# Two graph layers on one core: Q's first product ahead of fc_w's fourth, one block read by ScalarE's queue, and a reordered prologue

## The chip, the cores and the metric

The kernel runs on 1 core of one Trainium2 chip. The metric is the device time of one execution in microseconds. Three runs of the kernel before took 2433.7, 2435.32 and 2435.53 us; their median is 2435.32.

## The reference, cut to what matters

Two graph layers follow each other, on x of 64 x 256 x 512 and a 0/1 adjacency of 64 x 256 x 256, all in float32.

```python
# layer 0
feat_proj = feats @ fc_w.T + fc_b
q = feat_proj @ q_w.T + q_b;  k = feat_proj @ k_w.T + k_b
masked = (q + k.T) + (1 - adj) * -1e9
atten = softmax(leaky_relu(masked, 0.01))
x = atten @ feat_proj + feats
# layer 1, 8 heads of 64
Q, K, V = (x @ W + b for W, b in ((W_q, b_q), (W_k, b_k), (W_v, b_v)))
scores = Q K^T / 8 + (a_i + c_j + b_g) + log(adj + 1e-9)
out = softmax(scores) V + x          # a = x @ w_g[:512], c = x @ w_g[512:]
```

## The kernel before

**Groups and passes.** The 64 graphs are taken two at a time: a group is 2 graphs, 512 tokens, in four tiles of 128 tokens. `step(a, f, n)` is called 32 times and interleaves three groups: layer 1's attention of group a, layer 0 and the projections of group f, and the loads and the scalar logits of group n. Inside it, strings such as `F("pf.p4 pf.sum_10 send:1:0 fetch:1:0")` name methods in the order in which they are issued. The whole runs under a manual schedule, so on each engine the order of the program is the order of execution. There are 31 steps with attention and layer 0 (`attention_and_layer_0`), and a first one without attention (`features_first`).

**Products by seven.** The projections (class `Product`, L360) multiply 512 x 512 by 512 x 512 in 2 x 2 blocks with seven products in place of eight (Winograd's form). For this the blocks of the weights and of the tokens are added and subtracted first: `blocks_of_weights` (L285 to L288, on VectorE, once per weight) and `xsum:n` (L325) for the tokens. p1 to p7 are eight matmuls each; `keep_1` and its like copy a partial result from PSUM to SBUF on ScalarE, and `sum_00` to `sum_11` finish a block of the output on VectorE. Q's products are pq, K's pk, V's pv; pf is fc_w's product in layer 0, whose sums (L446) also scale by the softmax's denominators and add the residual. In pf the last product p4 adds to the PSUM bank of p7 after `sum_11` has read it.

**The way of x1.** Layer 0's result x1 stands with tokens on partitions and is needed with features on partitions. Four blocks (o, k) go through DRAM: `send:o:k` transposes 32 x 32 pieces on VectorE (L661) and writes xt to xd (L665), `fetch:o:k` reads it back into x1T with four transfers (L673), each write and read issued by SyncE. SyncE takes its instructions in order and waits for a write to land before it issues the reads of that block. Product pq.p1 needs block (0,0); `xsum:0` needs (0,1), `xsum:1` and `xsum:2` need (1,1), `xsum:3` and pq.p2 need (1,0); pq.p6 needs the first two sums.

**PSUM.** Pool ps has four banks for all products, sums and transposes; pool psc has two pairs of banks for the scores. A bank is given again when its last reader is done: pk.p1, for instance, takes the bank that the second oT copy (ScalarE, L774) reads.

**The prologue.** fc_w is loaded in one transfer by ScalarE's queue, q_w, k_w and fc_b as columns (`column`, L127: 512 pieces of 4 bytes each) by SyncE, then q_b, k_b, x and adj of group 0 and the three weights. `row_of_x` (L231) makes rows q_w fc_w and k_w fc_w on all partitions, from which VectorE takes the logits as dot products with x (`dot_q`, `dot_k`, L461). `transposed_weights` transposes fc_w (L148). `features_first` then transposes x (L591), computes feat_proj tile by tile (fp, L603), the softmax's weights e (L531 to L536), their sums (L544), and x1 (x1p, L621, L625). `constants_of_projections` (pc, L259) adds fc_b's part to Q's and V's bias; its four products of 32 rows lie in four column tiles of TensorE.

Of the kernel before, what the change touches and what calls it, by code (L numbers as in the profile page):

```python
# [10 lines left out]
F32 = mybir.dt.float32  # L11
I32 = mybir.dt.int32
AF = mybir.ActivationFunctionType
ALU = mybir.AluOpType
# [3 lines left out]
P = 128  # L18
# [7 lines left out]
def kernel(  # L26
# [133 lines left out]
    def fast():  # L160
        main = ExitStack()
        with main:
# [47 lines left out]
                nc.gpsimd.memset(ones[:, n, n : n + 1], 1.0)  # L210

            fc_nat = one.tile([P, T, D], F32, tag="xT", name="fc_nat")
            nc.scalar.dma_start(fc_nat, fc_w.rearrange("(c p) h -> p c h", p=P))
            qw_col = column(q_w.rearrange("a h -> (a h)"), "qw_col")
            kw_col = column(k_w.rearrange("a h -> (a h)"), "kw_col")
            fcb_col = column(fc_b, "fcb_col")
            qb = row(q_b, "qb")
            kb = row(k_b, "kb")
            x_0, adj_0 = load_x(0), load_adj(0)
            wq_sb = weights(W_q, "wq", wts)  # L220
            wk_sb = weights(W_k, "wk", wts)
            wv_sb = weights(W_v, "wv", wts)
            bq_col = column(b_q, "bq_col")
            wgc_row = row(w_g[D : 2 * D], "wgc_row")
            bv_col = column(b_v, "bv_col")

            def row_of_x(col, dst, name):

                pw = bank(name)
                for oc in range(NC):  # L230
                    nc.tensor.matmul(  # L231
                        pw, lhsT=col[:, oc : oc + 1].to_broadcast([P, P]), rhs=fc_nat[:, oc, :],
                        start=(oc == 0), stop=(oc == NC - 1),
                    )
                nc.scalar.copy(dst, pw)

            def constant():

# [14 lines left out]
            def constants_of_projections():  # L253


                pc = bank("pc")[:, 0:HALF]
                for n, (w, o) in enumerate(((wq_sb, 0), (wq_sb, 1), (wv_sb, 0), (wv_sb, 1))):
                    for c in range(NC):
                        nc.tensor.matmul(  # L259
                            pc[ts(n, RS), :], lhsT=fcb_col[:, c : c + 1].to_broadcast([P, RS]),  # L260
                            rhs=w[:, c, o * HALF : (o + 1) * HALF],
                            start=(c == 0), stop=(c == NC - 1), tile_position=(0, n * RS),
                        )
                rows = one.tile([P, HALF], F32, tag="st", name="pc_rows")
                nc.scalar.copy(rows, pc)
                pt = bank("pct")
                for m in range(2):
                    nc.tensor.transpose(pt[:, ts(m, P)], rows[:, ts(m, P)], ident)
                cols = pt[:, 0 : 2 * P].rearrange("p (m n r) -> p n m r", m=2, r=RS)
                for n, col in enumerate((bq_col, bq_col, bv_col, bv_col)):  # L270
                    half = col[:, ts(n % 2, 2)]
                    nc.vector.tensor_tensor(half, half, cols[:, n, :, 0], ALU.add)
                nc.vector.tensor_tensor(bv_col, bv_col, fcb_col, ALU.add)


            def block(w, r, c):
# [3 lines left out]
            def blocks_of_weights(w, name):  # L280


                a11, a12, a21, a22 = (block(w, f, o) for o, f in ((0, 0), (0, 1), (1, 0), (1, 1)))
                s = wts.tile([P, 3, 2, HALF], F32, tag=f"{name}_s", name=f"{name}_s")
                nc.vector.tensor_tensor(s[:, 1], a11, a21, ALU.subtract)  # L285
                nc.vector.tensor_tensor(a21, a21, a22, ALU.add)
                nc.vector.tensor_tensor(s[:, 0], a21, a11, ALU.subtract)
                nc.vector.tensor_tensor(s[:, 2], a12, s[:, 0], ALU.subtract)  # L288
                return {1: a11, 2: a12, 3: s[:, 2], 4: a22, 5: a21, 6: s[:, 0], 7: s[:, 1]}

            def blocks_of_tokens(xT, name):

# [173 lines left out]
            class Group:  # L466
# [113 lines left out]
                            )  # L580
                    nc.scalar.copy(self.yT[:, c, :], y)  # L581

                def features_first(self, fcT):

                    g = self.g
                    xT = one.tile([P, NC, TOK], F32, tag="qT", name=f"xT_{g}")
                    fp = one.tile([P, T, D], F32, tag="v", name=f"fp_{g}")
                    for t in range(T):
                        pt = bank(f"xTp_{g}_{t}")
                        for c in range(NC):  # L590
                            nc.tensor.transpose(pt[:, ts(c, P)], self.x[:, t, ts(c, P)], ident)  # L591
                        nc.scalar.copy(
                            xT[:, :, ts(t, P)], pt.rearrange("p (c n) -> p c n", c=NC)
                        )
                    self.queries()
                    for t in range(T):
                        if t == 2:
                            constants_of_projections()
                        if t == T - 1:
                            self.sums()  # L600
                        pp = bank(f"fp_{g}_{t}")
                        for c in range(NC):
                            nc.tensor.matmul(  # L603
                                pp, lhsT=xT[:, c, ts(t, P)], rhs=fcT[:, c, :],
                                start=(c == 0), stop=(c == NC - 1),
                            )
                        nc.scalar.copy(fp[:, t, :], pp)
                        if t == 2:
                            for name, wt in (("q", wq_sb), ("k", wk_sb)):
                                a_w[name] = blocks_of_weights(wt, name)  # L610
                        if t == 1:
                            self.weights(0)
                            self.weights(1)
                            self.add_eps()
                    self.recip()
                    self.begin()
                    for t in range(T):
                        gr, ic = divmod(t, TPG)
                        po = bank(f"x1p_{g}_{t}")
                        for j in range(TPG):  # L620
                            nc.tensor.matmul(  # L621
                                po, lhsT=self.e0[:, j, gr, ts(ic, P)], rhs=fp[:, gr * TPG + j, :],
                                start=(j == 0), stop=(j == TPG - 1),
                            )
                        nc.vector.scalar_tensor_tensor(  # L625
                            self.x[:, t, :], po, recip0[:, g, t : t + 1], self.x[:, t, :],
                            ALU.mult, ALU.add,
                        )
# [36 lines left out]
                    nc.sync.dma_start(d, xt)  # L665
                    self.d[o, k] = d

                def fetch(self, o, k):

                    src = self.d[o, k].rearrange("(a r) (q n) -> q r a n", r=B, q=P // B)  # L670
                    dst = self.x1T[:, o, k].rearrange("(q r) (a n) -> q r a n", r=B, a=P // B)
                    for q in range(P // B):
                        nc.sync.dma_start(dst[q], src[q])  # L673

                def x1t(self, t):

# [212 lines left out]
            def attention_and_layer_0(A, F, X):  # L889
# [10 lines left out]
                A("both:2")  # L900
                F("pf.sum_00 begin send:0:0 fetch:0:0 pf.p7 pf.p5")
                A("ratios_r:0 divide:0 complete:0 scores:3")
                F("pf.sum_11 send:1:1 pf.p3 pf.sum_01 send:0:1 fetch:1:1 fetch:0:1")
                A("factor:3:0 factor:3:1")
                F("pf.p4 pf.sum_10 send:1:0 fetch:1:0")
                A("both:3")
                F("pq.p1 pq.keep_1")
                A("attend:1 sums_1:1")
                F("pk.p1 pk.keep_1")

# [15 lines left out]
            def step(a, f, n):  # L926
# [17 lines left out]
                if a is not None:  # L944
                    attention_and_layer_0(A, F, X)
                else:
                    f.features_first(fcT)
                    F("pq.p1 pq.keep_1 pk.p1 pk.keep_1")
                F("xsum:0 xsum:1 xsum:2 pq.p6 keys:2 keys:3 keys:0 keys:1")
                X("load_x")  # L950
# [6 lines left out]
                if a is None:  # L957
                    a_w["v"] = blocks_of_weights(wv_sb, "v")
                A("divide:1")
                F("pk.sum_00 pq.p4")  # L960
                A("complete:1 store:1")
# [5 lines left out]
                if a is None:  # L967
                    a_w["fc"] = blocks_of_weights(fcT, "fc")
# [17 lines left out]
            with tc.manual_schedule(engines=ENGINES):  # L986
                f = Group(0)
                f.x, f.a = x_0, adj_0
                row_of_x(qw_col, wq_row, "pq_row")
                k_constant = constant()  # L990
                fcT = transposed_weights(fc_nat, wts, ps, nc.vector.tensor_copy)
                for t in range(T):
                    f.dot_q(t)
                f.adjt()
                row_of_x(kw_col, wk_row, "pk_row")
                k_constant()
                for t in range(T):
                    f.dot_k(t)
# [224 lines left out]
```

## Time and profile before

| | us |
|---|---|
| median of three runs | 2435.32 |
| the profiled execution | 2433.33 |
| its span, first to last instruction | 2431.6 |
| TensorE busy | 2395.3 |
| VectorE busy | 1876.4 |
| ScalarE busy | 1012.2 |
| first pq product of group 0 starts (chain) | 49.76 |

A profile line for a group of instructions gives the line of the kernel, the engine (PE is TensorE, PEld its weight loads, DVE VectorE, ACT ScalarE, POOL GpSimd, SP SyncE, with a q for transfers that the engine issues), the operation, output <- input, and the count. In a timeline the first two numbers are start and duration in us. In brackets stands the idle time before it and what ended it. In the list of waits, the engine and what it was about to do stand to the left of the arrow and what it waited for to the right; then follow the total, the number of times and the longest. The chain is the sequence of work and waits that ended last, followed back from the last instruction.

### The profile page before, as it was taken

How to read it: one execution, taken by the hardware profiler on the slowest of the kernel's cores; microseconds unless marked ns; L12 is line 12 of the kernel's file. 1: busy time of each engine (PE TensorE's matmuls, PEld its weight loads, DVE VectorE, ACT ScalarE, POOL GpSimd, SP SyncE). 2: the span in 40 equal slices, each digit the busy share in tenths (PEclk: the TensorE clock that was granted, in tenths of full speed). 3: DMA queues.
4: the chain of work that ended last, by engine and by line, in shares of the span. 5: the costliest groups of instructions: out<-in, count | busy, mean ns of one | idle time of the engine just before them, and what ended most of it. 6: DMA issues, size and time to landing. Idle time of an engine off the chain costs nothing.

```text
span 2431.6 us, 35923 instructions
## 1 busy us (share of the span) xinstructions
PE 2395.3 (99%) x13937; PEld 1916.5 (79%) x13937; DVE 1876.4 (77%) x3121; ACT 1012.2 (42%) x1771; POOL 140.0 (6%) x103
## 2 busy tenths in 40 slices
PE   8999999999999999999999999999999999999997
PEld 5778877888778878788877788777878777888776
DVE  4778777778777877777887778777778777788776
ACT  2444334444344434444434444334444434444343
POOL 0000000000000000000000000000000000000000
PEclk9999999999999999999999999999999999999999
DMA  4133322233212333123332223322233322233211
GB/s 126 27 70 83 83 61 52 57 79 83 70 48 57 74 83 81 57 51 61 83 83 70 47 57 76 83 75 51 54 70 83 83 61 51 55 83 83 70 45 31
DMA packets 519825, 163.99 MB, mean 67 GB/s; under 512 B 417760, under 2 KB 481248, under 8 KB 519648
## 3 DMA queue, kind: packets, MB, share of 16 engines
q1 hardware_dynamic: 516000, 160.18, 28.8%
q8 instruction: 112, 1.84, 0.3%
q10 hardware_dynamic: 3648, 1.44, 0.2%
q14 instruction: 65, 0.53, 0.1%
HBM read 95.43 MB, written 66.12 MB: 66 GB/s over the span
## 4 chain that ended last, share of the span: by engine, by line
PE 84%; DVE 4%; issue 4%; DMA 3%; POOL 2%; SPq 2%; ACT 0%; DVEq 0%; ACTq 0%
PE pv L360 16%; PE pk L360 15%; PE pq L360 15%; PE pf L360 11%; PE y L575 9%; PE sc L727 8%; PE oT L767 7%; POOL pf_s L440 2%; PE sm L783 2%; SPq L673 2%; DMA xd<-xt 2%; DMA x1T<-xd 1%; DVE x L446 1%; DVE t1b L325 1%; PE sm L544 1%
## 5 line engine op out<-in xcount | busy, mean ns | idle before, releaser
L747 DVE TENSOR_TENSOR e<-e,am 128x1024 f32<-128x1024 f32 x254 | 298.3, 1216 | 55.0 <-ACT e L741 55.0
L741 ACT ACTIVATE e<-sc,c 128x1024 f32<-128x1024 f32 x254 | 268.9, 1111 | 95.4 <-PE sc L727 95.4
L440 POOL TENSOR_TENSOR pf_s<-pf_s,x 128x512 f32<-128x512 f32 x93 | 139.1, 1496 | 2215.6 <-ACT pf_s L439 2143.7
L727 PE MATMUL sc<-qT,kT 64*128 64x256 f32 x2048 | 255.7, 389 | 0.0
L727 PEld LDWEIGHTS sc<-qT,kT 64*128 64x128 f32 x2048 | 187.3, 186 | 59.6 <-issue 42.1
L767 PE MATMUL oT<-e,v 128*64 128x256 f32 x2032 | 233.4, 382 | 0.0
L575 PE MATMUL y<-e,x 128*128 128x256 f32 x992 | 222.4, 382 | 0.0
L377 ACT ACTIVATE pq_s<-pq,bq_col 128x256 f32<-128x256 f32 x192 | 80.6, 471 | 328.4 <-PE pq L360 326.2
L575 PEld LDWEIGHTS y<-e,x 128*128 128x128 f32 x992 | 185.9, 190 | 34.3 <-issue 10.3
L767 PEld LDWEIGHTS oT<-e,v 128*64 128x64 f32 x2032 | 140.2, 137 | 85.5 <-issue 21.3
L439 ACT ACTIVATE pf_s<-pf,recip 128x256 f32<-128x256 f32 x186 | 78.1, 471 | 218.1 <-PE pf L360 157.5
L754 DVE TENSOR_TENSOR es<-e,e 128x1024 f32<-128x1024 f32 x126 | 151.9, 1205 | 1.1
L446 DVE SCALAR_TENSOR_TENSOR x<-pf,recip,pf_s 128x256 f32<-128x256 f32 x186 | 81.3, 479 | 73.2 <-POOL pf_s L440 73.2
L374 ACT COPY pk_s<-pk 128x512 f32<-128x512 f32 x96 | 56.3, 587 | 190.3 <-PE pk L360 135.2
L774 ACT COPY oTs<-oT 128x512 f32<-128x512 f32 x128 | 75.1, 587 | 129.1 <-PE oT L767 129.1
L360 PE MATMUL pq<-t1b,q_s 128*128 128x256 f32 x512 | 117.3, 382 | 9.7 <-DVE t1b L325 9.7
L581 ACT COPY yT<-y 128x512 f32<-128x512 f32 x124 | 72.7, 586 | 126.4 <-PE y L575 126.4
L360 PE MATMUL pf<-fcT,tb 128*128 128x256 f32 x496 | 120.4, 386 | 4.7 <-DVE x L446 3.5
L360 PE MATMUL pk<-x1T,wk 128*128 128x256 f32 x512 | 124.2, 385 | 0.0
L360 PE MATMUL pk<-t1b,wk 128*128 128x256 f32 x512 | 121.0, 379 | 1.2 <-DVE kT L388 1.2
L360 PE MATMUL pq<-x1T,wq 128*128 128x256 f32 x512 | 121.1, 379 | 0.7 <-DMA x1T<-xd 0.7
L360 PE MATMUL pv<-wv,t1b 128*128 128x256 f32 x512 | 121.1, 379 | 0.0
(159 smaller groups left out, 4357.3 us busy)
## 6 DMA issues: line engine op xcount, KB each, us to landing
x<-in_x_dram SPq DMA_DIRECT2D x32, 1024.0 KB, 5.7
out_dram<-osb SPq DMA_DIRECT2D x253, 128.0 KB, 3.1
xd<-xt SPq DMA_DIRECT2D x124, 256.0 KB, 2.0
x1T<-xd SPq DMA_DIRECT2D x496, 64.0 KB, 2.0
adj<-in_adj_dram SPq DMA_DIRECT2D x128, 128.0 KB, 4.8
qrow<-q SPq DMA_DIRECT2D x31, 256.0 KB, 4.2
fc_nat<-in_L_gnn_fc_w_dram ACTq DMA_DIRECT2D x1, 1024.0 KB, 5.9
wq<-in_L_gnn_W_q_dram SPq DMA_DIRECT2D x1, 1024.0 KB, 6.3
```

Source lines behind the costliest of these rows:

```text
L360: nc.tensor.matmul(o, lhsT=lk[:, ts(m, P)] if len(lk.shape) == 2 else lk[:, m], rhs=rk, start=(start and m == 0 and k == 0), stop=(m == 1 ...
L377: nc.scalar.activation(dst[:, m], src[:, m], AF.Identity, bias=self.bias[:, 2 * o + m : 2 * o + m + 1],)
L439: nc.scalar.mul(s[:, m], src[:, m], self.recip[:, TPG * k + m : TPG * k + m + 1])
L440: nc.gpsimd.tensor_tensor(s, s, self.out(o, k), ALU.add)
L446: nc.vector.scalar_tensor_tensor(dst[:, m], src[:, m], self.recip[:, TPG * k + m : TPG * k + m + 1], s[:, m], ALU.mult, ALU.add,)
L575: nc.tensor.matmul(y[:, ts(gr, N)], lhsT=self.x[:, gr * TPG + j, ts(c, P)], rhs=self.e0[:, j, gr, :], start=(gr == 0 and j == 0), stop=(gr ...
L727: nc.tensor.matmul(sc[:, par, pr, :], lhsT=self.kT[rows, 2 * hg + pr, ts(t, P)], rhs=self.qT[rows, 2 * hg + pr, ts(gr, N)], start=True, st ...
L741: nc.scalar.activation(e, sc, AF.Exp, bias=self.c[:, t : t + 1], scale=SCALE)
L747: nc.vector.tensor_tensor(ef, ef, self.am[:, jc, u // 2, :].unsqueeze(1).to_broadcast([P, 4, N]), ALU.mult,)
L754: nc.vector.tensor_tensor(self.esum[u], self.e[u, 0], self.e[u, 1], ALU.add)
L767: nc.tensor.matmul(oT[par * HD : (par + 1) * HD, pr, :], lhsT=self.v[:, gr * TPG + jc, ts(h, HD)], rhs=self.e[2 * gr + hg, jc][:, par, pr, :],
L774: nc.scalar.copy(self.oTs[gr][:, hg, :], po)
```

## The change

**In the steps with attention**, the order of issue becomes:

```diff
-                F("pf.sum_11 send:1:1 pf.p3 pf.sum_01 send:0:1 fetch:1:1 fetch:0:1")
+                F("pf.sum_11 send:1:1 pf.p3 pf.sum_01 send:0:1")
                 A("factor:3:0 factor:3:1")
-                F("pf.p4 pf.sum_10 send:1:0 fetch:1:0")
+                F("pq.p1 pq.keep_1 fetch_by_act:1:1 fetch:0:1 pf.p4")
                 A("both:3")
-                F("pq.p1 pq.keep_1")
+                F("pf.sum_10 send:1:0 fetch:1:0")
                 A("attend:1 sums_1:1")
```

`fetch_by_act` is `fetch` with the four transfers issued by ScalarE:

```diff
+                def fetch_by_act(self, o, k):
+                    self.fetch(o, k, nc.scalar)
+
-                def fetch(self, o, k):
+                def fetch(self, o, k, queue=nc.sync):
...
-                        nc.sync.dma_start(dst[q], src[q])
+                        queue.dma_start(dst[q], src[q])
```

On TensorE pq.p1 so stands before pf.p4; on ScalarE pq.keep_1 and four transfers stand before the copies of oT; on VectorE the sum es of `both:3` stands before pf.sum_10; on SyncE the four reads of block (1,1) are gone.

**In the prologue**, fc_w comes in four transfers of a chunk each. The vectors come as rows of 128 elements (three transfers with 4 pieces of 512 bytes) and are transposed by TensorE; q_b and k_b are loaded behind x and adj. Six matmuls of the identity stand first. The two rows share one loop over the chunks:

```diff
-            nc.scalar.dma_start(fc_nat, fc_w.rearrange("(c p) h -> p c h", p=P))
-            qw_col = column(q_w.rearrange("a h -> (a h)"), "qw_col")
...
+            for c in range(NC):
+                nc.scalar.dma_start(fc_nat[:, c, :], fc_w[ts(c, P), :])
...
+            rows_0 = rows_of_chunks([q_w[0], k_w[0], fc_b], "rows_0", "sms")
+            x_0 = load_x(0)
+            adj_0 = load_adj(0)
...
+            def columns(rows, cols, name):
+                n = rows.shape[0]
+                pt = bank(name)
+                nc.tensor.transpose(pt[:, 0:n], rows, ident[0:n, 0:n])
+                nc.vector.tensor_copy(cols, pt[:, 0:n])
...
+            def rows_of_x():
+                pq, pk = bank("pq_row"), bank("pk_row")
                 for oc in range(NC):
+                    for p, col in ((pq, qw_col), (pk, kw_col)):
+                        nc.tensor.matmul(
+                            p, lhsT=col[:, oc : oc + 1].to_broadcast([P, P]), rhs=fc_nat[:, oc, :],
+                            start=(oc == 0), stop=(oc == NC - 1),
+                        )
```

The products of `constants_of_projections` take the four column tiles in turn (the loop over chunks is now outside), and its transposes and additions are returned as `add_constants`, issued later. `blocks_of_weights` returns its four VectorE operations instead of issuing them. `features_first` then reads:

```diff
-                        nc.scalar.copy(
+                        nc.vector.tensor_copy(
                             xT[:, :, ts(t, P)], pt.rearrange("p (c n) -> p c n", c=NC)
...
+                    fcT = transposed_weights(fc_nat, wts, ps, nc.scalar.copy)
+                    for t in range(T):
+                        self.dot_q(t)
...
+                    product(0)
+                    self.queries()
+                    k_constant()
+                    for t in range(T):
+                        self.dot_k(t)
+                    self.adjt()
+                    product(1)
+                    columns(rows_1, cols_1, "cols_1")
+                    self.weights(0)
+                    self.weights(1)
+                    self.add_eps()
+                    product(2)
+                    add_constants = constants_of_projections()
+                    for name, wt in (("k", wk_sb), ("q", wq_sb)):
+                        for issue in blocks_of_weights(wt, name):
+                            issue()
+                    self.sums()
+                    product(3)
+                    add_constants()
                     self.recip()
                     self.begin()
+                    sums = blocks_of_weights(wv_sb, "v") + blocks_of_weights(fcT, "fc")
                     for t in range(T):
...
+                        for issue in sums[2 * t : 2 * t + 2]:
+                            issue()
```

Here `product(t)` is fp's tile t (four matmuls and a copy by ScalarE). The block sums of W_v and fc_w, eight operations on VectorE, so stand between the updates of x1 in place of two spots in the first step, where W_v's followed `copy:2` and fc_w's followed `dot_k:1`.

More of the change, by code (lines that the diff above doesn't have):

```diff
@@ L212, in fast, with rows_of_chunks @@
             fc_nat = one.tile([P, T, D], F32, tag="xT", name="fc_nat")
-            nc.scalar.dma_start(fc_nat, fc_w.rearrange("(c p) h -> p c h", p=P))
-            qw_col = column(q_w.rearrange("a h -> (a h)"), "qw_col")
-            kw_col = column(k_w.rearrange("a h -> (a h)"), "kw_col")
-            fcb_col = column(fc_b, "fcb_col")
+            for c in range(NC):
+                nc.scalar.dma_start(fc_nat[:, c, :], fc_w[ts(c, P), :])
+            def rows_of_chunks(vectors, name, tag):
+                t = one.tile([NC * len(vectors), P], F32, tag=tag, name=name)
+                for n, v in enumerate(vectors):
+                    nc.sync.dma_start(t[n * NC : (n + 1) * NC, :], v.rearrange("(c p) -> c p", p=P))
+                return t
+            rows_0 = rows_of_chunks([q_w[0], k_w[0], fc_b], "rows_0", "sms")
+            x_0 = load_x(0)
+            adj_0 = load_adj(0)
             qb = row(q_b, "qb")
             kb = row(k_b, "kb")
-            x_0, adj_0 = load_x(0), load_adj(0)
+            cols_0 = const.tile([P, 3 * NC], F32, tag="cols_0", name="cols_0")
+            cols_1 = const.tile([P, 2 * NC], F32, tag="cols_1", name="cols_1")
+            qw_col, kw_col, fcb_col = (cols_0[:, ts(n, NC)] for n in range(3))
+            bq_col, bv_col = (cols_1[:, ts(n, NC)] for n in range(2))
+            def columns(rows, cols, name):
[3 more added lines that the diff above has]
+                nc.vector.tensor_copy(cols, pt[:, 0:n])
             wq_sb = weights(W_q, "wq", wts)
@@ L222, in fast @@
             wv_sb = weights(W_v, "wv", wts)
-            bq_col = column(b_q, "bq_col")
+            rows_1 = rows_of_chunks([b_q, b_v], "rows_1", "sms1")
             wgc_row = row(w_g[D : 2 * D], "wgc_row")
-            bv_col = column(b_v, "bv_col")
-            def row_of_x(col, dst, name):
-                pw = bank(name)
+            def rows_of_x():
+                pq, pk = bank("pq_row"), bank("pk_row")
                 for oc in range(NC):
[L231 to L235, printed above, removed]
+                    for p, col in ((pq, qw_col), (pk, kw_col)):
[3 more added lines that the diff above has]
+                        )
+                nc.scalar.copy(wq_row, pq)
+                nc.scalar.copy(wk_row, pk)
             def constant():
@@ L256, in constants_of_projections @@
                 pc = bank("pc")[:, 0:HALF]
-                for n, (w, o) in enumerate(((wq_sb, 0), (wq_sb, 1), (wv_sb, 0), (wv_sb, 1))):
-                    for c in range(NC):
+                for c in range(NC):
+                    for n, (w, o) in enumerate(((wq_sb, 0), (wq_sb, 1), (wv_sb, 0), (wv_sb, 1))):
                         nc.tensor.matmul(
@@ L262, in constants_of_projections @@
                             start=(c == 0), stop=(c == NC - 1), tile_position=(0, n * RS),
+                            skip_group_check=True,
                         )
@@ L265, in constants_of_projections, with add @@
                 nc.scalar.copy(rows, pc)
[L266 to L273, printed above, removed]
+                def add():
+                    pt = bank("pct")
+                    for m in range(2):
+                        nc.tensor.transpose(pt[:, ts(m, P)], rows[:, ts(m, P)], ident)
+                    cols = pt[:, 0 : 2 * P].rearrange("p (m n r) -> p n m r", m=2, r=RS)
+                    for n, col in enumerate((bq_col, bq_col, bv_col, bv_col)):
+                        half = col[:, ts(n % 2, 2)]
+                        nc.vector.tensor_tensor(half, half, cols[:, n, :, 0], ALU.add)
+                    nc.vector.tensor_tensor(bv_col, bv_col, fcb_col, ALU.add)
+                return add
             def block(w, r, c):
@@ L284, in blocks_of_weights @@
                 s = wts.tile([P, 3, 2, HALF], F32, tag=f"{name}_s", name=f"{name}_s")
[L285 to L289, printed above, removed]
+                a_w[name] = {1: a11, 2: a12, 3: s[:, 2], 4: a22, 5: a21, 6: s[:, 0], 7: s[:, 1]}
+                return [
+                    lambda: nc.vector.tensor_tensor(s[:, 1], a11, a21, ALU.subtract),
+                    lambda: nc.vector.tensor_tensor(a21, a21, a22, ALU.add),
+                    lambda: nc.vector.tensor_tensor(s[:, 0], a21, a11, ALU.subtract),
+                    lambda: nc.vector.tensor_tensor(s[:, 2], a12, s[:, 0], ALU.subtract),
+                ]
             def blocks_of_tokens(xT, name):
@@ L581, in mix, with features_first @@
                     nc.scalar.copy(self.yT[:, c, :], y)
-                def features_first(self, fcT):
+                def features_first(self):
                     g = self.g
@@ L591, in features_first, with product @@
                             nc.tensor.transpose(pt[:, ts(c, P)], self.x[:, t, ts(c, P)], ident)
-                        nc.scalar.copy(
+                        nc.vector.tensor_copy(
                             xT[:, :, ts(t, P)], pt.rearrange("p (c n) -> p c n", c=NC)
                         )
-                    self.queries()
+                    fcT = transposed_weights(fc_nat, wts, ps, nc.scalar.copy)
                     for t in range(T):
[L597 to L600, printed above, removed]
+                        self.dot_q(t)
+                    def product(t):
                         pp = bank(f"fp_{g}_{t}")
@@ L607, in features_first @@
                         nc.scalar.copy(fp[:, t, :], pp)
[L608 to L614, printed above, removed]
+                    product(0)
[17 more added lines that the diff above has]
+                    add_constants()
                     self.recip()
                     self.begin()
+                    sums = blocks_of_weights(wv_sb, "v") + blocks_of_weights(fcT, "fc")
                     for t in range(T):
@@ L946, in step @@
                 else:
-                    f.features_first(fcT)
+                    f.features_first()
                     F("pq.p1 pq.keep_1 pk.p1 pk.keep_1")
@@ L956, in step @@
                 F("pq.sum_11 copy:0 pq.p3 copy:1 copy:2")
-                if a is None:
-                    a_w["v"] = blocks_of_weights(wv_sb, "v")
                 A("divide:1")
@@ L966, in step @@
                 X("dot_k:0 dot_k:1")
-                if a is None:
-                    a_w["fc"] = blocks_of_weights(fcT, "fc")
                 F("pk.sum_11")
@@ L988, in fast @@
                 f.x, f.a = x_0, adj_0
-                row_of_x(qw_col, wq_row, "pq_row")
-                k_constant = constant()
[L991 to L998, printed above, removed]
+                warm = bank("warm")
+                for n in range(6):
+                    nc.tensor.matmul(warm[:, 0:P], lhsT=ident, rhs=ident, start=True, stop=True)
+                columns(rows_0, cols_0, "cols_0")
+                rows_of_x()
+                k_constant = constant()
                 a, a_w = None, {}
```

## Prediction

> **What bounds the kernel now.** First the page's busy times: TensorE works all through the span. Then the shares of the chain that ended last, which say the same.
>
> ```profile
> PE 2395.3 (99%) x13937; PEld 1916.5 (79%) x13937; DVE 1876.4 (77%) x3121; ACT 1012.2 (42%) x1771; POOL 140.0 (6%) x103
> PE 84%; DVE 4%; issue 4%; DMA 3%; POOL 2%; SPq 2%; ACT 0%; DVEq 0%; ACTq 0%
> ```
>
> Only TensorE work or a TensorE wait can be won or lost. Third, the list of waits (total us, times, longest), for the products touched:
>
> ```profile
> DVE t1b L325 <- DMA x1T<-xd: 53.7, 33, 3.1
> PEld pf L360 <- DVE x L446: 17.1, 31, 0.6
> PE pq L360 <- DVE t1b L325: 9.7, 14, 1.4
> PE pq L360 <- DMA x1T<-xd: 0.7, 2, 0.5
> ```
>
> In each of 31 groups the weight load of pf's product 4 waits 0.55 us for VectorE (17.1/31); in 14 groups pq's product 6 waits for block sums, which wait for a transfer. Fourth, TensorE's and then SyncE's timeline of one group:
>
> ```profile
> 1011.97 1.99 PE L360 MATMUL pf<-fc_s,yT 128*128 128x256 f32 x8
> 1014.12 1.99 PE L360 MATMUL pf<-fcT,tb 128*128 128x256 f32 x8 [0.15 <-DVE x L446]
> 1015.95 1.89 PE L360 MATMUL pq<-x1T,wq 128*128 128x256 f32 x8
> 1017.77 3.67 PE L767 MATMUL oT<-e,v 128*64 128x256 f32 x32
> ```
>
> ```profile
> 1007.38 0.33 SPq L665 DMA_DIRECT2D xd<-xt  x1
> 1009.50 1.75 SPq L673 DMA_DIRECT2D x1T<-xd  x4
> 1014.84 1.84 SPq L665 DMA_DIRECT2D xd<-xt  x2
> 1017.10 4.11 SPq L673 DMA_DIRECT2D x1T<-xd  x8
> 1021.31 0.38 SPq L665 DMA_DIRECT2D xd<-xt  x1
> 1023.49 1.73 SPq L673 DMA_DIRECT2D x1T<-xd  x4
> ```
>
> From product 3's start to product 4's is 2.15 us; from 4 to pq's product 1, the same eight matmuls, 1.83. SyncE reads block (1,1), then (0,1) behind it, then writes and reads (1,0). Fifth, the chain over the first 60 us, in order of time:
>
> ```profile
> 0.79 5.87 DMA fc_nat<-in_L_gnn_fc_w_dram
> ...
> 6.79 5.57 PE pq_row L231 x8
> ...
> 14.41 3.64 PE pk_row L231 x8
> ...
> 27.33 4.54 PE pc L259 x32
> ...
> 49.76 1.73 PE pq L360 x8
> ```
>
> The prologue is TensorE's too, from 6.79 us on.
>
> **What the Trainium skill says.** "DMA: Bandwidth & Descriptors", Issuing engines are not separate DMA queues: a second issuing engine saves only the sequencer's issue time. Here that time is 1.75 us per block of four reads. The same page, Anatomy of one DMA: about 2 us is fixed and is mostly completion; the trace agrees (xd writes and x1T reads: median 2.0 us to landing). "TensorEngine Tiling (Array Packing)", Key Properties: column tiles work independently. The trace agrees: sm (L783), whose neighbours lie in different tiles, does 16 passes of 256 columns in 1.00 us, 62 ns each; pc (L259), with one tile's matmuls in a row, needs 142 ns. "TensorE: Matmul & The Clock Gate", Part 1: the clock rises after about 3.4 us of activity, in a free-running window. Here pq_row's loads are 0.86 us apart until 10.34 us, 3.6 after its start, and 0.43 from 10.9.
>
> **The change in the steady groups.** (a) *pq.p1 before pf.p4.* pq.p1 needs block (0,0), which in this group landed at 1012.85 (5.47 us after the write was issued; 5.3 to 6.5 over the groups), and its PSUM bank was freed long ago. It takes p4's place at the end of p3, 6.4 us after that write. p4's operand, sum_11 at VectorE, ends at 1014.07, before p4's new start at 15.5. Then 11.97 + 1.83 (as p4 to pq) + 1.73 (eight matmuls with their load prefetched) + 1.82 (pq to oT) puts oT at 1017.35 instead of 1017.77. 0.42 x 31 = **13.0 us gained**.
>
> (b) *Block (1,1) read by ScalarE.* ScalarE runs pq.keep_1 (0.84 us) from 1015.8, ends at 1016.65, waits for the write (issued 1014.84, 2.0 to landing) and issues four reads by 1018.6. Queued behind are the two oT copies at 1019.4 and 1021.1: 0.8 us of room, and the second copy, on which pk.p1's bank waits, stands 1.1 us behind the end of the first. With a write 3.8 to 4.1 us late (three groups, 715.33 to 719.16 for one) the issues end 1.9 to 2.1 later, about at the edge of that room. **0**; without the room every further us is a us of TensorE.
>
> (c) *Block (0,1) no longer behind (1,1) at SyncE.* Its reads start when its own write lands: 1018.35 instead of 1018.96; usually 0.4 us earlier, and 1.2 where the writes are late. So t1b starts about 0.4 to 1.2 us earlier, bounded by VectorE being free at about 1021. Product 6 comes 0.42 earlier by (a) and eats part of it. Of 9.7 us of waits I leave 4: **5.7 gained**.
>
> (d) *es before sum_10.* VectorE: factors end at 1018.5, es 1.2, sum_10 0.87, transpose 0.7: the write of (1,0) goes at about 1021.2, where SyncE's own backlog has it now in this group (1021.31); in a usual group it goes at 13.2 us after the first write and will go at 13.8. Landing of its reads: 5.3 to 5.5 later usually, up to 7.2, so 19.2 against pq.p2's start at 19.8. Some eight groups pass that by 0.1 to 1.1 us: **2 lost**. sm's first matmul waits for sum_10 too (p4's bank): ends at 13.1, needed at 13.5.
>
> **The prologue.** Rows by chunk: three small reads at SyncE in place of 4-byte columns, landing at about 3.8 us (1.8 + 2), a transpose and a copy (0.7), so both rows start at about 4.5 and not 6.79. 16 passes of 0.43 are 6.9 us; if four are at 0.86, 8.6: end 11.4 to 13.1. The six warm matmuls may shorten it; I count none. x_0, which landed at 15.09 behind the columns, is issued at 2.3 instead of 3.41 and lands near 9 (2 MB at the 300 to 385 GB/s that the transfer view shows, plus 2 us). xTp and pfc are paced by eight copies of 0.62 (2.48/4), 4.8 us: fp starts at 16.2 to 18.0, not 20.36. From there: four fp at 3.44, qrow 0.48, pc at 62 ns x 32 = 2.0 (was 4.54), sm 0.57, pct 0.44, rc 0.11 and 0.1 for columns: 17.5, with the wait for pc's copy (0.44) gone behind fp. x1p at 33.7 to 35.6, was 40.51. But VectorE now has eight block sums of 0.7 between the x1 updates (1.4 + 0.75 per tile against TensorE's 2.16), with 1.6 us lost at its end: pq.p1 at 44.5 to 46.5, was 49.76. Middle: **4.3 gained**. The constants (five small operations) delay the reciprocal by 0.9, hidden by x1p's first 1.7 us. The sums of fc taken out of group 0's keys free TensorE's wait of 1.24 us at 75.17 (pk <- kT): **1.2 gained**. The weights' transfers issue earlier; pc needs them at 27 at the earliest, and wv lands at 27.26 even now.
>
> **Sum.** 13.0 + 5.7 - 2 + 4.3 + 1.2 = 22.2. Against the profiled execution: 2433.33 (span 2431.6 and 1.7 around it) to 2411.1. Its time lies 2.0 under the median 2435.32, so **2413** for the median.
>
> **Rivals.** *ScalarE blocks* (0.17): if one issue costs what the last stores cost there (2.66 us for three, 0.89 each), four take 3.55 and the room in (b) is used up; each of seven groups with late writes pays 1 to 2 us, some 10 in all: 2423. For it: ScalarE's order is fixed. Against: fc_nat's issue took 0.48 there, and those stores have 128-byte pieces. *VectorE takes over* (0.13): sum_10 ends 0.4 us later than worked out, sm waits for it and (a) is given back: only 5.5 from the prologue and little else, 2428. For it: VectorE is without a gap from 1016.2. Against: the same instructions, with es hidden before. *Slower* (0.10): the last block, (1,0), comes late for pq.p2 in every group, as its write starts later and two queues share the engines. It decides once the reads land 0.6 us over the estimate; each us beyond costs 31, and break-even is at 0.8 beyond that (24.2/31). Landing 2 us later than estimated gives 1.4 x 31 = 43 lost against 24 won: 2454. For it: landings scatter by 1.9 us. Against: 26 of the 31 landings lie within 0.5 us. *Does nothing* (0.05): block (0,0) lands after p3's end (1 us later than now), pq.p1 waits as p4 did, and the prologue's gain is eaten by pq.p2: 2435.
>
> **How the numbers follow.** Forecast 0.55, its own range 2404 to 2420 (none or all of the remaining waits, prologue 3 to 7). With ScalarE and VectorE, both faster, 0.85; within 0.2% (4.9 us, about what this measurement can tell from no change) 0.05; slower 0.10. The range 2402 to 2430 takes in the forecast, both faster rivals and little else: 0.8.
>
> **What would show it.** Right: pf's wait for VectorE gone from the list; p3 to pq 1.83 us; shortest distance of two groups 73.7 us instead of 74.12 (chain, pq at 1098.72 to 1172.84); t1b's wait under 20 us; pq.p1 of group 0 near 45.5; pc near 2. Wrong: oT copies that start after ScalarE's reads; sm waiting for x L446; pq waiting for x1T in most groups; xTp waiting for x_0.

## The result and the profile after

The changed kernel takes **2411.72 us** (median of six runs, 2410.60 to 2413.88), against 2434.80 (2433.70 to 2435.53) for the kernel before beside it: a ratio of 0.9906, with a 95% interval of 0.9893 to 0.9919. The forecast was 2413 within 2402 to 2430. The profiled execution took 2410.6 with a span of 2408.8; the forecast for it was 2411.1.

The page of the kernel after, first the busy times and then the shares of the chain that ended last:

```profile
PE 2387.0 (99%) x13951; PEld 1921.1 (80%) x13951; DVE 1881.2 (78%) x3123; ACT 1012.5 (42%) x1771; POOL 140.3 (6%) x103
PE 92%; DVE 3%; DMA 2%; issue 1%; SPq 1%; POOL 1%; ACT 0%; DVEq 0%
```

TensorE still sets the time, more than before: its share of the chain went from 84% to 92%. The list of waits of the kernel after (total us, times, longest):

```profile
DVE t1b L354 <- DMA x1T<-xd: 31.8, 43, 2.1
ACT oTs L821 <- DMA x1T<-xd: 31.5, 11, 3.0
PEld sm L830 <- DVE x L475: 11.5, 30, 0.4
...
PE pq L389 <- DMA x1T<-xd: 2.8, 5, 0.9
PE pq L389 <- DVE t1b L354: 2.2, 3, 1.0
PE cols L237 <- DMA rows<-in_L_gnn_b_v_dram: 0.9, 1, 0.9
```

Three things are to be seen. The weight load of product 4 no longer stands in the list as waiting for VectorE (it was 31 times, 17.1 us). TensorE's waits for block sums fell from 9.7 us to 2.2, and those for a block itself rose from 0.7 to 2.8. The last line is new and belongs to the prologue. TensorE's timeline in one group of the kernel after shows the new order (start and duration in us):

```profile
999.59 1.99 PE L389 MATMUL pf<-fc_s,yT 128*128 128x256 f32 x8
1001.42 1.89 PE L389 MATMUL pq<-x1T,wq 128*128 128x256 f32 x8
1003.15 1.89 PE L389 MATMUL pf<-fcT,tb 128*128 128x256 f32 x8
1004.97 3.67 PE L814 MATMUL oT<-e,v 128*64 128x256 f32 x32
```

From product 3 to oT it is 1.83 + 1.73 + 1.82 = 5.38 us; before it was 5.80. SyncE's timeline of the same group, and then ScalarE's:

```profile
1002.46 1.84 SPq L709 DMA_DIRECT2D xd<-xt  x2
1006.48 1.75 SPq L720 DMA_DIRECT2D x1T<-xd  x4
1009.00 0.34 SPq L709 DMA_DIRECT2D xd<-xt  x1
```

```profile
1003.35 0.84 ACT L406 ACTIVATE pq_s<-pq,cols 128x256 f32<-128x256 f32 x2 [2.33 <-PE pq L389]
1004.67 2.47 ACTq L720 DMA_DIRECT2D x1T<-xd  x4
1007.24 0.59 ACT L821 COPY oTs<-oT 128x512 f32<-128x512 f32 x1 [3.04 <-DMA x1T<-xd]
1008.69 0.59 ACT L821 COPY oTs<-oT 128x512 f32<-128x512 f32 x1 [0.87 <-PE oT L814]
```

The reads of block (0,1) start at SyncE at 1006.48, as soon as their own write has landed, while ScalarE is still issuing those of (1,1). ScalarE's four end at 1007.14; the first oT copy starts at 1007.24 here, 0.2 us later than in most groups, and the second has 0.87 us of slack in front of it. The group shown is one of the unfavourable ones: ScalarE's four issues take 2.47 us here, and 1.76 to 1.82 in 29 of the 31 groups.

**Where the 22.8 us of span went.** From the first write of xd to that of the last group the trace has 2220.31 us (before 2238.64): the steady part gained 18.3. The first write stands at 107.29 (before 111.82): the prologue and the first group gained 4.5. The rest, to the end, is equal (81.2 and 81.1).

This is one profile against one, and the steady part scatters. Seven of the profiled executions below have the changed order of the steady groups as it stands; theirs takes 2220.3 to 2225.4 us, on average 2222.3, and the changed kernel's own is the shortest. Two have the old order, with 2238.6 and 2240.2. By these averages the steady part gains 17.1 us, about one less than the pair above shows.

### The profile page after: what moved, and what is told of

Read it like the earlier page. It is cut to its first block, busy times and chain, and to the rows that moved or that the text cites. A ratio compares the mean times of both kernels' runs of the same rounds, so it can differ in the third digit from the quotient of the medians.

```text
span 2408.8 us, 35925 instructions
## 1 busy us (share of the span) xinstructions
PE 2387.0 (99%) x13951; PEld 1921.1 (80%) x13951; DVE 1881.2 (78%) x3123; ACT 1012.5 (42%) x1771; POOL 140.3 (6%) x103
## 4 chain that ended last, share of the span: by engine, by line
PE 92%; DVE 3%; DMA 2%; issue 1%; SPq 1%; POOL 1%; ACT 0%; DVEq 0%
PE pv L389 16%; PE pk L389 16%; PE pq L389 15%; PE pf L389 14%; PE sc L774 10%; PE y L604 9%; PE oT L814 8%; PE sm L830 2%; DMA xd<-xt 1%; DVE x L475 1%; DMA x1T<-xd 1%; POOL pf_s L469 1%; PE sm L573 1%; DVE e L794 0%; SPq L720 0%
## 5 line engine op out<-in xcount | busy, mean ns | idle before, releaser
L604 PEld LDWEIGHTS y<-e,x 128*128 128x128 f32 x992 | 185.9, 190 | 34.3 <-issue 10.3
L406 ACT ACTIVATE pq_s<-pq,cols 128x256 f32<-128x256 f32 x192 | 80.7, 471 | 255.9 <-PE pq L389 255.9
L475 DVE SCALAR_TENSOR_TENSOR x<-pf,recip,pf_s 128x256 f32<-128x256 f32 x186 | 81.2, 478 | 73.1 <-POOL pf_s L469 73.1
L389 PE MATMUL pv<-wv,t1b_c 128*128 128x256 f32 x512 | 121.0, 379 | 0.0
L389 PE MATMUL pq<-t1b,wq 128*128 128x256 f32 x512 | 120.9, 379 | 0.0
```

The costliest lines, as they stand in the source:

```text
L389: nc.tensor.matmul(o, lhsT=lk[:, ts(m, P)] if len(lk.shape) == 2 else lk[:, m], rhs=rk, start=(start and m == 0 and k == 0), stop=(m == 1 ...
L406: nc.scalar.activation(dst[:, m], src[:, m], AF.Identity, bias=self.bias[:, 2 * o + m : 2 * o + m + 1],)
L475: nc.vector.scalar_tensor_tensor(dst[:, m], src[:, m], self.recip[:, TPG * k + m : TPG * k + m + 1], s[:, m], ALU.mult, ALU.add,)
L604: nc.tensor.matmul(y[:, ts(gr, N)], lhsT=self.x[:, gr * TPG + j, ts(c, P)], rhs=self.e0[:, j, gr, :], start=(gr == 0 and j == 0), stop=(gr ...
```

## The experiments

Each ratio is against the kernel before, run in the same series.

**The two parts alone.** The first kernel has the prologue of before, and the new order of the steady groups with ScalarE's reads.

```diff
-                F("pf.sum_11 send:1:1 pf.p3 pf.sum_01 send:0:1 fetch:1:1 fetch:0:1")
+                F("pf.sum_11 send:1:1 pf.p3 pf.sum_01 send:0:1")
...
-                F("pf.p4 pf.sum_10 send:1:0 fetch:1:0")
+                F("pq.p1 pq.keep_1 fetch_by_act:1:1 fetch:0:1 pf.p4")
...
-                F("pq.p1 pq.keep_1")
+                F("pf.sum_10 send:1:0 fetch:1:0")
```

> The prologue of the kernel before with the new order of the steady groups. Theory: the two parts don't meet, and the groups alone bring what the trace of the changed kernel shows between the first and the last write of xd, 18.3 us: 2434.8 - 18.3 = 2416.5; pq.p1 of group 0 still starts at 49.8. Rival: part of the groups' gain came with the prologue (fc_w's block sums gone from VectorE, transfers shifted against each other): more than 2420.

Measured 2417.82, ratio 0.9926 (0.9910 to 0.9943). The second kernel is the changed one with these lines put back.

> The changed kernel's prologue with the old order of the steady groups. Theory: 4.5 us less than before, 2430.3: 3.0 at pq.p1 (46.7 instead of 49.8) and about 1.4 from block sums that no longer hold up K's sum in group 0. Rival: the earlier start is given back at the first transfer of the next group: within 1 us of before.

Measured 2431.84, ratio 0.9985 (0.9978 to 0.9992). By medians the steady order so brings 18.1 us and the prologue 4.1; the sum, 22.2, is close to the 23.1 of both together, so the parts add within the scatter. Nearly four fifths of the gain come from three lines of order and the small helper that they use. No run separates the parts of the prologue from each other.

**Product 4 first again, the reads left with ScalarE.** This undoes step (a) alone.

```diff
-                F("pq.p1 pq.keep_1 fetch_by_act:1:1 fetch:0:1 pf.p4")
+                F("pf.p4 fetch_by_act:1:1 fetch:0:1 pq.p1 pq.keep_1")
```

> The changed kernel with pf.p4 ahead of pq.p1 again; ScalarE issues its four reads before pq.keep_1, so that they start as in the changed kernel. Theory: product 3 to product 4 is 2.15 us again, 0.42 x 31 = 13 us more: 2424.7, with the waits for block (0,1) still gone. Rival: TensorE's wait in front of p4 was slack that later waits take up: less than 6 us more, under 2418.

Measured 2419.23, ratio 0.9934 (0.9917 to 0.9950): 7.5 us above the changed kernel by medians, 8.5 by span. The list of waits of this kernel:

```profile
PEld pf L389 <- DVE x L475: 17.1, 31, 0.6
...
PE pq L389 <- DVE t1b L354: 1.3, 3, 0.7
```

The wait of 17.1 us is back to the tenth, and product 6 starts at the earliest 16.81 us after the group's first write, against 16.40: 0.41 in each of 31 groups, 12.7 us, as step (a) has it. But TensorE's waits further on are smaller here. Measured at the y product near a group's end, the groups exceed their earliest start by 4.4 us in sum; in the changed kernel by 9.2, and by 9.2 to 14.3 in the seven executions with its order. So a group that is 0.42 faster meets its transfers 0.42 earlier, and about 4.8 of 12.7 us, in this pair of profiles, go into waits. Neither theory had that: one expected the full 13, the other less than 6.

**ScalarE's reads given back to SyncE,** with pq.p1 first: steps (b) and (c) undone alone.

```diff
-                F("pq.p1 pq.keep_1 fetch_by_act:1:1 fetch:0:1 pf.p4")
+                F("pq.p1 pq.keep_1 fetch:1:1 fetch:0:1 pf.p4")
```

> The changed kernel with block (1,1) read by SyncE again, ahead of (0,1); pq.p1 stays ahead of pf.p4. Theory: the 0.42 us per group stay, the waits for block (0,1) come back: t1b starts 0.4 us later in usual groups, where product 6 now comes 0.42 earlier and has 0.2 left, and 1.2 later where writes are late: 6 to 10 us more than the changed kernel, 2418 to 2422. Rival: the second queue does nothing, since all transfers share the same engines: 2412.

Measured 2423.14, ratio 0.9957 (0.9940 to 0.9973): 11.4 above by medians, 9.4 by span. SyncE's timeline of one group of this kernel, then its list of waits:

```profile
1005.86 1.84 SPq L709 DMA_DIRECT2D xd<-xt  x2
1008.20 4.25 SPq L720 DMA_DIRECT2D x1T<-xd  x8
1012.54 0.38 SPq L709 DMA_DIRECT2D xd<-xt  x1
```

```profile
PEld pq L389 <- DVE t1b L354: 22.0, 24, 2.0
...
PE pq L389 <- DVE t1b L354: 14.0, 14, 1.6
```

SyncE issues eight reads in a row, and those of block (0,1) are the second four. Over the groups they start 11.61 us after the first write, on average, and VectorE's first block sum, which waits for them, starts at 15.43; in the changed kernel it is 11.10 and 14.73. That is enough: TensorE waits 14.0 us for block sums where the changed kernel waits 2.2. Summed over the groups, product 6 is 17.3 us behind its earliest start, against 4.1 in the changed kernel and 4.1 to 8.4 in the seven executions with its order. The write of block (1,0) hardly moves (14.09 on average, against 14.01). So with product 1 ahead, but without the second issuing engine, the change keeps about half of its 23 us.

**sum_10 ahead of es**, to undo step (d):

```diff
-                A("both:3")
                 F("pf.sum_10 send:1:0 fetch:1:0")
+                A("both:3")
```

> The changed kernel with pf.sum_10 and the write of block (1,0) ahead of es (both:3) again. Theory: block (1,0) is written 0.5 to 1.2 us earlier, so the waits of pq.p2 (some 3.5 us in all) go; es then ends at 13.8 us after the first write, where sm's fifth matmul stands at 13.8: 2 to 3 us less, 2409. Rival: sm waits for es 0.2 to 0.4 us in every group, 6 to 12 us more, 2416 to 2421.

Measured 2412.49, ratio 0.9907 (0.9891 to 0.9924): the same as the changed kernel. Neither the theory nor the rival came true, though each saw something. Its list of waits:

```profile
PE pq L389 <- DVE t1b L354: 6.7, 11, 1.3
...
PEld sm L830 <- DVE es L801: 0.4, 1, 0.4
```

No product waits for block (1,0) any more, which step (d) said would win 2 us; and sm waits for es once only, 0.4 us, where the other theory expected it in every group. But product 6 waits 6.7 us instead of 2.2: the early write of (1,0) now goes 12.9 us after the group's first write, while the reads of (0,1), begun at 11.0, are still under way. That these two collide would explain it, but this is argued and not shown: summed over the groups product 6 is 9.5 us behind its earliest start here, and between 4.1 and 8.4 in the executions that leave this order alone.

**Product 5 ahead of product 2.** The same wait for block (1,0), taken away in another way: product 5, which doesn't need the block, moves in front of product 2, which does, and K's product 2 moves behind product 3.

```diff
-                F("pq.p2 pq.sum_00 pq.p5 pk.p2")
+                F("pq.p5 pq.p2 pq.sum_00 pq.p3")
...
-                F("pq.sum_11 copy:0 pq.p3 copy:1 copy:2")
+                F("pq.sum_11 copy:0 pk.p2 copy:1 copy:2")
```

> The changed kernel with Q's products in the order 6 7 5 2 3 in place of 6 7 2 5, and K's product 2 behind them. Product 2, which needs block (1,0), starts 1.73 us later, product 5 needs only ScalarE's copy. Theory: pq.p2's waits for x1T (about 3.5 us over seven groups) go and nothing else comes: 2408.5. Rival: VectorE's sums, or the bank for K's product 2, come late and TensorE waits for them: 2412 or more.

Measured 2408.94, ratio 0.9898 (0.9882 to 0.9915): 2.8 under the changed kernel by medians, 4.0 by span. TensorE's timeline of one group of this kernel, products 6 and 7, then 5, then 2:

```profile
1009.15 3.72 PE L389 MATMUL pq<-t1b,q_s 128*128 128x256 f32 x16
1012.71 1.89 PE L389 MATMUL pq<-t1b,wq 128*128 128x256 f32 x8
1014.44 1.89 PE L389 MATMUL pq<-x1T,wq 128*128 128x256 f32 x8
```

Product 2 now starts 1.7 us later, behind work that was due anyway, and TensorE's wait for a block is gone from the list. Summed over the groups, the y product is 5.8 us behind its earliest start, below all of the seven executions with the changed order (9.2 to 14.3). So the wait that step (d) named is a real loss, and it can be removed; that the time falls by about its size fits, but the runs of the two kernels overlap (2406.6 to 2412.2 here, 2410.6 to 2413.9 there).

**The row of b_v**, the new wait of the prologue. The transpose of b_q and b_v moves behind the third feat_proj tile.

```diff
                     product(1)
-                    columns(rows_1, cols_1, "cols_1")
                     self.weights(0)
                     self.weights(1)
                     self.add_eps()
                     product(2)
+                    columns(rows_1, cols_1, "cols_1")
```

> The changed kernel with the transpose and copy of b_q's and b_v's rows moved from ahead of weights(0) to behind product(2). Theory: TensorE and VectorE don't wait until 27.2 us for that transfer; TensorE wins the 0.9 us of its wait, VectorE 1.6, and VectorE's chain ends the prologue: pq.p1 at 45.1 to 45.9 instead of 46.7, 0.9 to 1.6 us less in all, 2410.5. Rival: pc and the sums of the weights wait for the same queue, pq.p1 stays at 46.7.

Measured 2410.28, ratio 0.9898 (0.9882 to 0.9915). Its interval overlaps the changed kernel's; the place shows it better than the total. First the chain of the kernel after, then the chain of this one:

```profile
17.31 9.89 DMA rows<-in_L_gnn_b_v_dram
27.33 0.20 PE cols L237
27.53 3.63 PE fp L631 x8
31.16 1.86 PE pc L280 x32
...
46.73 1.73 PE pq L389 x8
```

```profile
22.36 6.87 PE fp L631 x16
29.23 0.15 PE cols L237
29.38 1.86 PE pc L280 x32
...
44.95 1.73 PE pq L389 x8
```

A row of 2 KB is issued at 17.31, behind the three weights of 1 MB each, lands at 27.20, and the transpose that waits for it holds the feat_proj tile behind it. Without this wait pq.p1's first matmul comes 31.55 us after the last weight load of the rows has ended, and the same 31.55 in the combined kernel below; in the nine executions with it, 31.75 to 35.55, on average 1.25 more. Of the 1.8 us between these two chains 0.6 is another thing: the clock rose 1.6 us earlier in this execution, and the last weight load of the rows ended at 13.24 instead of 13.88.

**The clock at the start.** The six matmuls of the identity were given no gain in the prediction. One kernel has seven, and two more between the columns' transpose and the rows, so that TensorE has no gap; another has none.

```diff
-                for n in range(6):
+                for n in range(7):
                     nc.tensor.matmul(warm[:, 0:P], lhsT=ident, rhs=ident, start=True, stop=True)
                 columns(rows_0, cols_0, "cols_0")
+                for n in range(2):
+                    nc.tensor.matmul(warm[:, 0:P], lhsT=ident, rhs=ident, start=True, stop=True)
```

> The changed kernel with seven matmuls of the identity ahead of the columns and two between the columns' transpose and the rows (six ahead in the changed kernel), so that TensorE has no gap of 0.26 us there. Theory: [...]the rows' loads come 0.43 us apart from 6.9 on instead of 10.3: rows end near 13.0 instead of 14.7, pq.p1 at most 1 us earlier since the transfer of b_v's row still holds product(2) at 27.3. Rival: the clock rises near 10.3 whatever is issued before, and the three extra matmuls delay the rows by 0.5.

> The changed kernel without the six matmuls of the identity. Theory: they bring nothing where they are, since TensorE then stands still twice before the rows: the loads of the rows come 0.43 us apart only from 8.6 to 10.4 us on, as with them, and the whole is within 1 us of the changed kernel. Rival: they start the window, and without them the clock rises 1.5 us or more later: rows end after 14.5, pq.p1 0.5 to 1 later.

Measured 2411.88, ratio 0.9911 (0.9894 to 0.9927), with the gap filled, and 2412.14, ratio 0.9903 (0.9887 to 0.9920), without any: neither differs from the changed kernel. The weight loads of the rows show TensorE's clock: they stand 0.85 us apart at first and 0.43 once it has risen. First the kernel after, then the same loads with the gap filled:

```profile
8.63 0.34 PEld L251 LDWEIGHTS pq_row<-fc_nat,cols 128*128 128x128 f32 x1 [0.52 <-issue]
9.48 0.34 PEld L251 LDWEIGHTS pk_row<-fc_nat,cols 128*128 128x128 f32 x1 [0.52 <-issue]
...
10.69 0.19 PEld L251 LDWEIGHTS pq_row<-fc_nat,cols 128*128 128x128 f32 x1 [0.24 <-issue]
11.12 0.19 PEld L251 LDWEIGHTS pq_row<-fc_nat,cols 128*128 128x128 f32 x1 [0.24 <-issue]
```

```profile
6.14 0.19 PEld L251 LDWEIGHTS pk_row<-fc_nat,cols 128*128 128x128 f32 x1 [0.24 <-issue]
6.57 0.19 PEld L251 LDWEIGHTS pk_row<-fc_nat,cols 128*128 128x128 f32 x1 [0.24 <-issue]
```

With the gap filled the clock was up from the first row on, and pq.p1 started at 44.48 instead of 46.57. In the second execution with the gap filled, the combined kernel below, it rose at 7.4 us, also earlier than in eight of the nine with the gap. But its rise scatters (see the last section), and the medians of the runs don't show a gain. Whether filling the gap shortens the kernel on average stays open.

**The adjacency behind the weights.** In the kernel after, x_0 landed at 12.81 us instead of near 9, and the four adjacency loads behind it held SyncE from 2.29 to 13.33. Here they stand last in the prologue's loads.

```diff
             x_0 = load_x(0)
-            adj_0 = load_adj(0)
...
             wgc_row = row(w_g[D : 2 * D], "wgc_row")
+            adj_0 = load_adj(0)
```

> The changed kernel with adj of group 0 loaded behind the weights, b_q, b_v and w_g instead of ahead of q_b and the weights. Theory: adj's small pieces are what held fc_w's last chunks, x_0 and all behind them: x_0 lands by 9.5 instead of 10.8 to 13.9, b_v's row by 21, pq.p1 has no wait for it and starts at 44.5 to 45.5, 1 to 2 us less in all. Rival: x_0 and fc_w hold each other up without adj as well, and adj now lands too late for VectorE's transpose at 24: pq.p1 at 46.5 or later.

Measured 2414.99, ratio 0.9920 (0.9904 to 0.9937). The chain of this kernel:

```profile
1.83 7.71 DMA x<-in_x_dram
...
19.99 3.68 DMA adj<-in_adj_dram
```

x_0 lands at 9.54, so it was the adjacency, four transfers of 128 KB, that delayed it; but nothing waits for x_0 at that time, as the rows' matmuls, which stand ahead of x_0's first reader, run until 12.0 here, where the clock happened to be up from their start, and longer in every other execution. The adjacency itself now lands at 23.67, VectorE waits 2.2 us for it, and the runs show no gain: the median is 4.0 above the changed kernel's in the same series (2410.96). The cause of the late x_0 is so found, and the delay cost nothing.

**The three edits together**: product 5 first, b_v's columns later, the gap filled; beside it the changed kernel again.

> The changed kernel with the three edits of the earlier runs together: Q's product 5 ahead of 2, the columns of b_q and b_v behind product(2), matmuls of the identity in the gap. Theory: they act at different places and add up: 3 (waits of pq.p2), 1.5 (wait for b_v's row), 0 to 1.5 (clock): 2406 beside 2411.7 for the changed kernel, pq.p1 of group 0 at 43.5 to 45. Rival: the starts of groups shift and the waits for block (0,1) take the gain: 2409 or more.

> The changed kernel itself, once more beside the others: 2411.7 within 2 us. pq.p1 of group 0 between 45.1 and 48.8, as in the runs that share its prologue; pq's waits for x1T and t1b together 4 to 9 us.

The combined kernel measured **2407.57** (2406.96 to 2408.10), ratio 0.9887 (0.9871 to 0.9904); the changed one again 2410.96 (2409.25 to 2411.94), ratio 0.9900 (0.9883 to 0.9916). The combined kernel's time lies between the 2406 of the theory and the 2409 of the rival. The intervals of the ratios overlap, but all four runs of the combined kernel are shorter than the shortest of the changed kernel's ten. It is the best kernel of the study, 3.4 us under the changed one.

## Why the prediction was right

The time, 2413 against 2411.72, is nearer than the steps are: the mechanism held in both parts, while errors of 1 to 2 us in single terms cancelled, which is luck. By the prediction's own steps:

**(a) pq.p1 before pf.p4: 13.0 predicted.** Right in place and size: product 4's wait is gone, p3 to pq is 1.83 us, and product 6 comes 0.41 earlier in 31 groups, 12.7 us. The shortest distance of two groups is 73.70 us, where 73.7 was named. What the step did not say is that an earlier TensorE also waits more for the transfers behind: undone alone it costs 7.5 to 8.5, and not 12.7.

**(b) ScalarE's reads: 0 predicted.** Right. The list's 31.5 us are no loss in themselves, since oT is not there before 12.0 us. The first oT copy came 0.2 to 0.7 us late in seven groups, a sign that the prediction had named for being wrong; it cost nothing, since the second copy, the one a PSUM bank hangs on, starts between 13.68 and 13.72 in 30 of 31, and later only where pq.p1 itself was late. The 2 us to landing come from the trace, which has a median of 2.0 for these transfers when SyncE issues them and 2.1 when ScalarE does; the section of the skill that the prediction names beside it gives its figure for transfers issued by gpsimd.

**(c) Block (0,1) sooner: 5.7 predicted.** Right in mechanism, and somewhat small in size. Product 6's lateness over the groups fell from 12.4 to 4.1 us in the pair of profiles, which is 8.3; on average over the executions with either order (12.4 and 14.8 before, 4.1 to 8.4 after) it fell by 7.2. The step started from the 9.7 us of the list, which leaves out weight loads that come late. Its sign, t1b's wait under 20 us, did not come: it is 31.8 us, against 53.7 before. That wait is VectorE's, and TensorE's behind it is what counts.

**(d) es before sum_10: 2 lost predicted.** Right. The write of (1,0) goes at 13.99 us (13.8 was worked out), and product 2's lateness beyond product 6's rose from 2.4 to 4.7 us in sum. The combined and product-5 kernels won it back.

These make 12.7 + 8.3 - 2.3 = 18.7 for the steady part, where the pair of traces has 18.3 and the prediction had 16.7. With the averages it is 12.7 + 7.2 - 2.3 = 17.6, where the traces have 17.1.

**The prologue: 4.3 and 1.2 predicted.** pq.p1 starts at 46.73 in the chain, just outside the 44.5 to 46.5 given, so 3.0 were won. Three terms were mis-sized. The rows start at 5.05 and not 4.5: the columns' transpose waits for the last of the three small rows, which was to land at 3.8. The six warm matmuls ahead of it have little part in that, as the rows start at 4.79 without them:

```profile
4.54 0.25 PE L237 MATMUL cols<-ident,rows 12*128 12x12 f32 x1 [0.16 <-DMA rows<-in_L_gnn_fc_b_dram]
```

The clock rose at 10.3, after about six slow passes where four were allowed for, so the rows' matmuls run until 14.55 and not until 11.4 to 13.1. And the transpose of b_q and b_v was given 0.1 and no wait. The weights' transfers do issue 0.9 us earlier (14.56 against 15.45), but b_v's row stands behind them, lands at 27.20, and the tile behind its transpose waits 0.9 us; the kernel with the columns later shows that this wait costs 1.25 on average. x_0 landed at 12.81 instead of near 9, without a cost. The column tiles in turn were right: pc takes 1.86 us for 32 passes (2.0 predicted, 4.54 before). So x1p starts at 37.26, 1.7 us outside the 33.7 to 35.6 given; that pq.p1 misses its range by 0.2 only is luck, since from x1p to pq.p1 it takes 9.5 us where 10.8 were allowed. Counted to the first write of xd, 4.5 were won, which leaves 1.5 for the sums of fc taken out of group 0 (1.2 predicted); TensorE's wait of 1.2 us for K's sum is gone from the list.

**The rivals.** *ScalarE blocks* fell: four issues took 1.8 us in most groups and 2.9 at most, not 3.55, and no second copy was late for them. *VectorE takes over* fell. Its sign is there: sm's weight load waits for the sum in 30 groups, 11.5 us in all. But before it waited as long for es:

```profile
PEld sm L783 <- DVE es L754: 11.9, 31, 0.4
```

These loads are at most 0.4 us late, and sm's matmuls start 13.57 us after the first write in 28 groups, where it was 13.99 before.

*Slower* fell: block (1,0) made product 2 late by 0.5 to 1.0 us in five groups, and by 0.1 or less in the others. *Does nothing* fell too, with one group to show for it: there block (0,0) landed 6.94 us after its write was issued, and pq.p1 waited 0.65.

The kernel's own excess of median over profile was taken as 2.0 us and was 1.1; that, and 0.5 of work, is the whole error of the total: in this pair of profiles the steady part won 1.6 more than worked out and the prologue, with the fc sums, 1.0 less.

## What to carry to other kernels

Where one engine works all the time and waits a little for another in every round, put in front of the waiting product one whose operands are long there; then look at what the saved time makes late next, since a transfer that lands when it did before takes a part back. A second issuing engine is worth what the transfers queued behind the first one's wait start earlier, where someone waits for just those: here half a us per group, and half of the gain. A small load that something waits for belongs ahead of the large ones, or its reader later.

## What the runs showed of the hardware

**Half a microsecond of issue is half of the gain.** The Trainium skill, "DMA: Bandwidth & Descriptors", Issuing engines are not separate DMA queues, states that issuing from several engines saves only the sequencer's time to initiate the transfer, usually small beside the transfer itself. The runs fit that, and show what it can be worth: of 1.75 us of issue per block, 0.5 us appear as an earlier start of the next reads (11.61 to 11.10), 0.7 as an earlier start of the sum that waits for them (15.43 to 14.73), and 9.4 us by span over 31 groups, 0.30 each.

**The clock rose 3.5 to 6 us after TensorE began to work without a gap.** Nine executions began with the same six warm matmuls, two gaps of up to 0.3 us around the columns' transpose, and the rows from 4.9 to 5.1 us. In eight of them the rows' loads went from 0.85 to 0.43 us apart at 8.6, 8.6, 8.7, 10.1, 10.2, 10.3, 10.3 and 11.0 us, 3.5 to 5.9 us after the rows began. Without the warm matmuls, with the rows from 4.8, it was 9.2, 4.4 later. With the gaps filled, so that the work runs from 1.45 on, it was 5.7 and 7.4, 4.3 and 6.0 later. The ninth, with the adjacency loaded last, is the exception: its rows were fast from 5.1 on, so there the warm matmuls were enough in spite of the gaps. "TensorE: Matmul & The Clock Gate", Part 1, has a free-running window of about 3.4 us that does not start with the kernel. An estimate from that figure, one whole window after a wait of up to another, is 3.4 to 6.8 us after the work begins, and the eleven other executions lie in it. Among the nine with the same start the rows' matmuls end between 12.0 and 14.8 us. So up to 2.8 us in a prologue are chance, and an edit that is worth less can't be read from one profile.
